# Row products of a Winograd convolution without column sums, with halved GpSimd sums and a planner that knows of the shared SBUF port

## The chip, the cores and the metric

The kernel runs on one core of a Trainium2 chip. The metric is device time in microseconds, from several runs of the compiled program; the time before is 2768.17 us, the median of 3 runs that lie between 2763.59 and 2770.75. The profile is one execution on the chip; times in the text that look like 533.33 are microseconds from the start of its span. Engines are named as in the profile: PE is TensorE, PEld its weight loads, DVE is VectorE, ACT is ScalarE, POOL is GpSimd, and SP is the engine that issues most DMAs.

## The reference, cut to what matters

There are 4 images of 256 channels and 48 x 48 pixels, in fp32. Two layers follow each other, each added to its input.

```python
# layer 0
h   = relu(bn(conv3x3(group_norm(x)) + conv_b))      # 256 -> 256 channels
q,k,v = split(qkv_w @ h + qkv_b)                     # 8 heads of 32
a   = softmax(q.T @ k * 32**-0.5) @ v                # over all 2304 pixels
x   = x + proj_w @ a + proj_b
# layer 1
g   = group_norm(x)
guidance = conv3x3(g, W_cat)                         # 45 channels
outs = [g]
for i, d in enumerate((1, 6, 12, 24, 36)):
    w = softmax(guidance[:, 9*i:9*i+9], axis=1)      # one 3x3 filter per pixel
    outs.append(sum(shift(g, d, tap) * w[:, tap] for tap in range(9)))
y   = W_scale @ concat(outs)                         # 1536 -> 256 channels
x   = x + batch_norm(y)                              # statistics over all images
```

## The kernel before, in words

**Stages.** The program first runs the conv and the q, k, v products of image 0 alone. Then, for each image, it runs the attention (some 350 us), and after it a stage in which layer 1 of this image (`dynamic_filters`, L1429 on) and the conv and q, k, v products of the next image are interleaved on TensorE. After image 3 layer 1 runs with work left over from image 2 in place of a next conv (`late`), and then the output is normalized and written. In the profile the interleaved stages are about 508 to 819, 1174 to 1486 and 1842 to 2154 us, and the last stage begins at about 2503.

**Order of instructions.** The order on every engine is the order in which the Python code issues instructions; nothing is moved later. To find a good order the code keeps a planner, `clock` (class `Clock`): an estimated time for each engine, advanced by an assumed duration at each instruction. `drive` holds several generators (the steps of layer 1) with a due time for each, and issues the first one that is due; where none is due it takes one step of the generator `other`, the next image's conv, if the time in `need[0]` has come. `run(ns)` takes conv steps worth that many nanoseconds. `either` puts a sum on DVE or POOL, whichever the planner expects to be done first; `moved` does the same for a copy on ACT or DVE.

**The conv.** Image 0 uses `conv`: rows are transformed by Winograd's F(4,3) down the columns of the image, which leaves six row products i = 0..5, each a matmul sum over 2 input halves and 3 horizontal taps. Images 1 to 3 use `Blocks` and `conv_blocks`: the same six row products, in the order `ORDER = (1, 2, 3, 4, 0, 5)`, and within each one F(2,3) along the row. So a tile (i, o), with o an output half, has four column products j of 2 matmuls each, 288 columns wide (L1139). Their inputs are column sums made by `along` from the row sums `v[i]` (four sums of 576 elements per partition for each i); those of rows 1, 2 and 3 are put on POOL, those of 4, 0 and 5 on either engine. The row sums `v[i]`, 1200 elements per partition, are all made by POOL (`sum`, L979): those of rows 1 and 2 in `stage0`, issued as the attention ends, the others in the generator `rest`. After each tile the four products are put together out of PSUM: ACT copies the first to `one`, DVE makes `two` with the second, and the third and fourth are added, by DVE from PSUM or by ACT and either engine. `after` adds pairs of row products, and ACT applies the batch norm and relu into `hid`. The transformed weights are made once, under image 0's conv (`Made`), stored in DRAM (`u_d`) and read a tile at a time by SP into one of three ring buffers (`taken`).

**End of the attention.** The exponentials `p` of a unit of queries are summed for the softmax by DVE (`acc`), a part of them by accumulating DMAs (`extra`). In the last unit of an image DVE adds `extra` to `acc` at step 15 and the exponentials of step 16 after that; the last step's go to TensorE directly. `close` sums `acc` over the partitions on TensorE, DVE makes reciprocals of them (two transposes) and scales the result, and `project` multiplies the last chunk by `proj_w` (L1412, tile `pp`). Only for image 3 are five idle "warm" matmuls issued between.

**Start of layer 1.** DVE adds the residual to `pp` and takes statistics, TensorE sums them over groups, and `gn` is normalized in place, half of the channels by DVE (L641) and half by ACT (L1963). Ahead of that ACT loads the square root's table, and after the square root the exponential's.

**Layer 1, per chunk of 8 rows.** `weights` makes the softmaxed filters; `far` does the four large dilations as matmuls with a banded matrix `amat`, which DVE fills by three predicated copies (L1660), from data that `own` and `xT` bring in order; `near` does dilation 1 by products on DVE, added up by POOL (L1759); `mixes` applies `W_scale` (L1854).

Of the kernel before, what the change touches and what calls it, by code (L numbers as in the profile page):

```python
# [17 lines left out]
P = 128  # L18
# [39 lines left out]
def conv_preact_kernel(  # L58
# [487 lines left out]
    with tc.tile_pool(name="w", bufs=1) as wpool, tc.tile_pool(  # L546
# [145 lines left out]
        class Clock:  # L692
# [3 lines left out]
            def __init__(self):  # L696
                self.t = dict.fromkeys(("PE", "DVE", "ACT", "POOL"), 0.0)

            def __call__(self, engine, ns, *after):

                self.t[engine] = max(self.t[engine], *(a + 150.0 for a in after), 0.0) + ns
                return self.t[engine]

# [27 lines left out]
        STEPS = [(i, j) for i, _ in TILES for j in (1, 2, 0, 3)]  # L731

        def taken(t):

            i, o = TILES[t]
            at = 1024 * ((t + 2) % 3)
            u = ring[:, at : at + 1024]
            nc.sync.dma_start(out=u, in_=u_d[i, o])
            return u.rearrange("p (h j c) -> p h j c", h=NH, j=4)

        class Made:
# [20 lines left out]
            def convert(self):  # L762
# [5 lines left out]
                for o in range(NH):  # L768
                    t = four[:, at + NH * 4 * P * o : at + NH * 4 * P * (o + 1)]
                    f = t.rearrange("p (h j c) -> p h j c", h=NH, j=4)  # L770
                    of = self.u[i][:, :, :, o * P : (o + 1) * P]
# [179 lines left out]
        class Blocks:  # L951


            def __init__(self, b, gn):
# [19 lines left out]
                self.of = {1: v[:, :z]}  # L974
                pad = gn.rearrange("p h r w -> p (h r w)")
                self.pad = [pad[:, z * j : z * (j + 1)] for j in range(2)]
                self.end = {}
                self.passed = set()

            def sum(self, out, x, y, op):  # L980
                nc.gpsimd.tensor_tensor(out, x, y, op)
                return clock("POOL", 2800)

            def stage0(self):
# [3 lines left out]
                nc.scalar.mul(v[5], d[1], 4.0)  # L988
                self.sum(v[0], d[4], v[0], ALU.subtract)
                self.sum(v[5], d[3], v[5], ALU.subtract)  # L990
                self.sum(v[1], v[0], v[5], ALU.add)
                self.along(1)
                self.sum(v[2], v[0], v[5], ALU.subtract)
# [7 lines left out]
            def rest(self):  # L1001
# [3 lines left out]
                for out, x, y, op in (  # L1005
                    (3, d[4], d[2], ALU.subtract), (6, v[6], v[4], ALU.subtract),
                    (4, v[3], v[6], ALU.subtract), (3, v[3], v[6], ALU.add),
# [19 lines left out]
                for i, after in ((4, 2), (0, 3), (5, 4)):  # L1027
# [13 lines left out]
            def hidden(self, hid):  # L1041
# [3 lines left out]
                    {2: hid[:, :z], 3: hid[:, z:], 4: self.pad[0], 0: self.pad[1], 5: self.pad[0]}  # L1045
                )

            def along(self, i, js=(1, 2, 0, 3)):
# [3 lines left out]
                for j in js:  # L1052
# [3 lines left out]
                    if i in ORDER[:3]:  # L1056
                        nc.gpsimd.tensor_tensor(to, d[x], d[y], op)
                        self.end[i, j] = clock("POOL", 1400)
                    else:
                        self.end[i, j] = either(to, d[x], d[y], op)  # L1060

        def either(out, a, c, op, *after):

            part = 0.5 if len(out.shape) == 2 and out.shape[-1] == XN else 1.0
            if clock.t["POOL"] + 1400 * part <= clock.t["DVE"] + 1000 * part:
                nc.gpsimd.tensor_tensor(out, a, c, op)
                return clock("POOL", 1400 * part, *after)
            nc.vector.tensor_tensor(out, a, c, op)
            return clock("DVE", 1000 * part, *after)

        def conv_blocks(b, psum_tile, blocks, pool, hid):
# [6 lines left out]
            results, last = [], [0.0]  # L1078
# [16 lines left out]
            def before(i, o):  # L1095

                s12, d12, s34, d34 = (blocks.held[:, j, o] for j in range(4))
                if i == 0:
                    t = spare.pop(0)
                    axpy(t, s34, -4.0, s12)  # L1100
                    relu(o, 2, t, clock("DVE", 700))
                    either(s12, s12, s34, ALU.subtract)
                elif i == 5:
                    t = spare.pop(0)
                    axpy(t, d34, -2.0, d12)
                    relu(o, 1, t, clock("DVE", 700))
                    axpy(d12, d34, -8.0, d12)
                    clock("DVE", 700)

            def target(i, o):  # L1110

                if i in (1, 3):
                    return blocks.first[o]
                if i in (2, 4):
                    return blocks.held[:, 1 if i == 2 else 3, o]
                return spare.pop(0)

            def after(i, o, y):

                s12, d12, s34, d34 = (blocks.held[:, j, o] for j in range(4))  # L1120
                if i in (2, 4):
                    s, d = (s12, d12) if i == 2 else (s34, d34)
                    either(s, y, blocks.first[o], ALU.add)
                    either(d, blocks.first[o], y, ALU.subtract)
                elif i in (0, 5):
                    relu(o, i and 3, y, either(y, y, s12 if i == 0 else d12, ALU.add))
# [1251 lines left out]
```

## Time and profile before

| | |
|---|---|
| median of 3 runs | 2768.17 us (2763.59 to 2770.75) |
| the profiled execution | 2768.08 us, of which the span is 2766.3 us |
| busy in the span | PE 2596.0, DVE 2142.2, ACT 1796.7, POOL 741.7 us |
| PE in the interleaved stages | 287.11 of 311, 289.84 of 312, 285.68 of 312 us |
| PE in the last stage, 2503 to 2767 | 212.90 of 264 us |
| DVE in the interleaved stages | 208.42, 207.02, 226.25 us |
| POOL in the interleaved stages | 159.43, 159.31, 163.91 us |
| mean granted TensorE clock | 0.982 |

In the tables of the profile a line gives the source line, the engine, what is written and read, and after the bar the busy time, the mean duration in ns and the idle time of the engine just before, with what ended it. In a timeline the first two columns are start and duration in us; several like instructions may be merged into one row (x8), and a bracket gives the idle time before and what ended it. A matmul of the program stands as two matmul records.

### The profile page before, as it was taken

To read this page: it belongs to the slowest core of one execution; us is meant where nothing else is said; L and a number is where in the kernel's file an instruction comes from. 1 tells how busy PE (TensorE), PEld (TensorE's weight loads), DVE (VectorE), ACT (ScalarE), POOL (GpSimd) and SP (SyncE) were. 2 spreads that over 40 slices of the span, in tenths; PEclk is the share of its full clock that TensorE was granted. 3 is DMA by queue.
4 is the path that set the end of the run, shared out by engine and by line. 5 is a ranking of instruction groups with operands and counts; after the bars stand their busy time and mean duration, and the time that the engine had idled before them with its cause. 6 is when DMAs were issued, how large, how long until landed. Compare 5 with 4: busy or idle time off the path is not lost. (4 is left out here: it accounts for less than half of the span.)

```text
span 2766.3 us, 42026 instructions
## 1 busy us (share of the span) xinstructions
PE 2596.0 (94%) x16820; PEld 1089.6 (39%) x16820; DVE 2142.2 (77%) x2045; ACT 1796.7 (65%) x2242; POOL 741.7 (27%) x641
## 2 busy tenths in 40 slices
PE   6999999889999999988999999998999999999994
PEld 5632222455562222345554222244555222234452
DVE  7778888777739988858765988885876988885476
ACT  3478888633449988843346888883445988873244
POOL 5200100456420100065550001016654010000352
PEclk9999999999999999999999999999999999999997
DMA  4704444323242444422333444442335344442465
GB/s 172 219 18 98 109 98 103 81 69 99 78 92 58 105 99 95 109 77 76 89 70 67 92 98 102 99 94 71 86 83 133 93 93 100 94 92 63 118 180 183
DMA packets 135979, 273.64 MB, mean 99 GB/s; under 512 B 56040, under 2 KB 97936, under 8 KB 134880
## 3 DMA queue, kind: packets, MB, share of 16 engines
q0 software_dynamic: 25952, 135.74, 21.5%
q1 hardware_dynamic: 109824, 135.14, 18.4%
q8 instruction: 134, 2.20, 0.4%
q14 instruction: 69, 0.57, 0.1%
HBM read 112.12 MB, written 36.04 MB: 54 GB/s over the span
## 5 line engine op out<-in xcount | busy, mean ns | idle before, releaser
L1340 DVE TENSOR_TENSOR acc<-acc,p 128x2048 f32<-128x2048 f32 (+1 forms) x572 | 1061.2, 1855 | 122.7 <-ACT p L1304 73.1
L1304 ACT ACTIVATE p<-se 128x1536 f32<-128x1536 f32 x648 | 938.7, 1449 | 0.1
L1295 PE MATMUL so<-q,k 32*128 32x512 f32 (+1 forms) x1440 | 726.4, 592 | 19.6 <-ACT p L1303 18.9
L1295 PE MATMUL se<-q,k 32*128 32x512 f32 (+1 forms) x4320 | 735.0, 592 | 0.0
L1324 PE MATMUL num<-p,vT 128*32 128x512 f32 (+1 forms) x5760 | 706.2, 560 | 4.6 <-ACT p L1304 2.4
L1303 ACT ACTIVATE p<-so 128x512 f32<-128x512 f32 x648 | 388.4, 599 | 193.8 <-PE se L1295 82.8
L1759 POOL TENSOR_TENSOR near<-near,prod 128x768 f32<-128x768 f32 x192 | 351.8, 1833 | 357.2 <-DVE prod L1754 347.6
L1295 PEld LDWEIGHTS so<-q,k 32*128 32x128 f32 x1440 | 216.1, 183 | 535.0 <-ACT p L1303 496.3
L1324 PEld LDWEIGHTS num<-p,vT 128*32 128x32 f32 x5760 | 134.5, 108 | 479.2 <-issue 444.3
L1344 POOL DMA_DIRECT2D ring<-p x124 | 105.5, 851 | 779.8 <-ACT p L1304 464.8
L1754 DVE TENSOR_TENSOR prod<-wb,pad 128x768 f32<-128x768 f32 x192 | 181.7, 953 | 68.5 <-ACT wb L1741 48.9
L1854 PE MATMUL py<-far,wsc 128*128 128x384 f32 x704 | 234.5, 487 | 0.0
L1295 PEld LDWEIGHTS se<-q,k 32*128 32x128 f32 x4320 | 226.7, 183 | 5.4 <-ACT p L1304 4.1
L1741 ACT COPY wb<-ws 128x384 f32<-128x384 f32 x216 | 109.0, 509 | 174.7 <-DVE prod L1754 146.4
L1462 ACT COPY far<-far 128x512 f32<-128x512 f32 x92 | 97.4, 1105 | 143.4 <-PE far L1688 142.0
L1342 POOL DMA_DIRECT2D ring<-p x32 | 17.9, 558 | 640.8 <-ACT p L1304 481.5
L1854 PEld LDWEIGHTS py<-far,wsc 128*128 128x128 f32 x704 | 131.9, 190 | 89.8 <-issue 1.8
L1489 PE MATMUL pg<-pad,wcat 128*45 128x384 f32 x864 | 151.7, 498 | 3.5 <-ACT lg L1547 2.1
L1219 PE MATMUL pq<-hid,wqkv 128*128 128x384 f32 x384 | 130.2, 497 | 7.6 <-ACT hid L1089 5.4
L1688 PE MATMUL far<-amat,xT 64*128 64x256 f32 x576 | 86.0, 416 | 18.3 <-DVE amat L1660 18.3
L1219 PEld LDWEIGHTS pq<-hid,wqkv 128*128 128x128 f32 x384 | 73.6, 194 | 60.6 <-ACT hid L1089 7.0
L1340 DVE TENSOR_TENSOR acc<-p,p 128x2048 f32<-128x2048 f32 x36 | 82.3, 2285 | 19.6 <-ACT p L1304 19.6
(305 smaller groups left out, 2711.1 us busy)
## 6 DMA issues: line engine op xcount, KB each, us to landing
ring<-p POOLq DMA_DIRECT2D x156, 768.0 KB, 5.7
ws<-w_d SPq DMA_DIRECT2D x216, 192.0 KB
ring<-u_d SPq DMA_DIRECT2D x36, 512.0 KB
pad<-in_x SPq DMA_DIRECT2D x14, 1152.0 KB
xst<-in_x POOLq DMA_DIRECT2D x36, 192.0 KB, 3.6
x_d<-pad SPq DMA_DIRECT2D x36, 192.0 KB
u_d<-pad SPq DMA_DIRECT2D x12, 512.0 KB
y_d<-y SPq DMA_DIRECT2D x14, 384.0 KB
```

The source lines that it names most:

```text
L1219: nc.tensor.matmul(pq[:, :CH], wqkv[:, i, s, g * P : (g + 1) * P], hid[:, i, cols], start=(i == 0), stop=(i == NH - 1),)
L1295: nc.tensor.matmul(dst[:, at : at + n], k_[r, g, m * P : (m + 1) * P], q[r, g, q0 : q0 + n], start=True, stop=True,)
L1303: nc.scalar.activation(p[:, 0, :], s1, AF.Exp, scale=QS)
L1304: nc.scalar.activation(p[:, 1:, :], s3, AF.Exp, scale=QS)
L1324: nc.tensor.matmul(st["num"][r, at : at + n], vT[:, m, g * P + j * D : g * P + (j + 1) * D], p[:, j, at : at + n], start=(m == 0 and not s ...
L1340: nc.vector.tensor_tensor(st["acc"][:, js], other[:, js], p[:, js], ALU.add)
L1344: nc.gpsimd.dma_start(out=extra, in_=p[:, 1:], accum_op=ALU.add)
L1489: nc.tensor.matmul(pg[64 * s : 64 * s + NG, :CH], wcat[:, ii, k, :], shifted(ii, cc, k // 3 - 1, k % 3 - 1), start=(i == 0 and k == 0), st ...
L1741: nc.scalar.copy(pw[:, :CH], fetched[c, k][0])
L1754: nc.vector.tensor_tensor(prod.rearrange("p h (r w) -> p h r w", w=WW), wb, src, ALU.mult)
L1759: nc.gpsimd.tensor_tensor(cat, cat, prod, ALU.add)
L1854: nc.tensor.matmul(py[c][:, o, :CH], wsc[:, n * NH + i, o * P : (o + 1) * P], rhs, start=(n == 0 and i == 0), stop=(n == order[-1] and i = ...
```

## The change

- **Planner.** `Clock` remembers POOL's last sums and the last DVE instruction that excludes them. `alone` gives the time at which DVE can start such an instruction; `both` books it and pushes POOL's later sums back. `either`, a layer-1 softmax product, the copies of `own` and those into `amat` now use it.
- **Half sums.** POOL's row sums and its sums in `near` are issued as two instructions, one per channel half.
- **Whole rows.** For rows 1 and 2 (`WHOLE`) there are no column sums: a tile has two halves of the output, each 6 matmuls (2 input halves x 3 taps) straight from `v[i]`. ACT copies row 1's products to `first`; DVE makes row 2's sum and difference with them from PSUM. Their weights are three per tile instead of four. The row sum `v[3] = d[4] - d[2]` moves to the front of `stage0`. The other rows' column sums get other buffers, may begin one row product earlier, and row 3's may go to either engine; one relu of row 0 is held back because of that.
- **End of the attention.** In the last unit steps 16 and 17, `acc` and `extra` are all summed by TensorE; DVE's two last additions go. The warm matmuls are issued for every image.
- **Start of layer 1.** The normalization is issued in two halves with conv steps between; the exponential's table is loaded at the first `weights`. Three clears move from POOL to DVE. In the last stage the last `pp` lies in two banks of another pool.
- **amat.** The three predicated copies are issued together.

```diff
@@ Clock
+            def alone(self, *after):
+                at = max(self.t["DVE"], *(a + 150.0 for a in after), 0.0)
+                return next((end for start, end in self.sums if start <= at < end), at)
+
+            def both(self, ns, *after):
+                at = self.alone(*after)
+                self.t["DVE"] = at + ns
+                self.held = at, at + ns
...
@@ Blocks
             def sum(self, out, x, y, op):
-                nc.gpsimd.tensor_tensor(out, x, y, op)
-                return clock("POOL", 2800)
+                for h in range(NH):
+                    nc.gpsimd.tensor_tensor(out[:, h], x[:, h], y[:, h], op)
+                    end = clock("POOL", 1400)
+                return end
@@ stage0
+                self.sum(v[3], d[4], d[2], ALU.subtract)
                 self.sum(v[0], d[4], v[0], ALU.subtract)
                 self.sum(v[5], d[3], v[5], ALU.subtract)
-                self.sum(v[1], v[0], v[5], ALU.add)
-                self.along(1)
-                self.sum(v[2], v[0], v[5], ALU.subtract)
+                for i, op in zip(WHOLE, (ALU.add, ALU.subtract)):
+                    end = self.sum(v[i], v[0], v[5], op)
...
@@ along
-                    if i in ORDER[:3]:
-                        nc.gpsimd.tensor_tensor(to, d[x], d[y], op)
-                        self.end[i, j] = clock("POOL", 1400)
-                    else:
-                        self.end[i, j] = either(to, d[x], d[y], op)
+                    self.end[i, j] = either(to, d[x], d[y], op)
@@ either
-            if clock.t["POOL"] + 1400 * part <= clock.t["DVE"] + 1000 * part:
+            if clock.t["POOL"] + 1300 * part <= clock.alone(*after) + 900 * part:
...
@@ conv_blocks
+                    if whole:
+                        half = slice(TJ * j, TJ * (j + 1))
+                        pairs = [
+                            (u[:, h, kx], blocks.v[i][:, h, half, kx : kx + WW])
+                            for h in range(NH) for kx in range(3)
+                        ]
...
+                        if i == ORDER[0]:
+                            nc.scalar.copy(first, m)
+                        else:
+                            tt(blocks.held[:, 0, o, cols], m, first, ALU.add)
+                            tt(blocks.held[:, 1, o, cols], first, m, ALU.subtract)
...
@@ attention
-                if end and m == NT - 1:
-                    sums(u, p, True, False)
+                if end and m >= NT - 2:
+                    sums(u, p, m == NT - 2, m == NT - 1)
+                    if m == NT - 2:
+                        sums(u, state[u]["acc"], False, False)
+                        sums(u, extra, False, False, 1)
...
-                sums(u, state[u]["acc"], u < last, True)
-                if u == last and b == B - 1:
+                if u < last:
+                    sums(u, state[u]["acc"], True, True)
+                else:
                     busy(ps_a.tile([P, 512], F32, tag="one", name="warm"), 5)
@@ dynamic_filters
-                nc.gpsimd.memset(t, 0.0)
+                nc.vector.memset(t, 0.0)
...
+                    yield lambda: clock.t["DVE"] - AHEAD
                     for t in range(3):
-                        yield lambda: clock.t["DVE"] - AHEAD
                         nc.vector.copy_predicated(
...
-                    nc.gpsimd.tensor_tensor(cat, cat, prod, ALU.add)
-                    end = clock("POOL", 1800, end)
+                    for h in range(NH):
+                        nc.gpsimd.tensor_tensor(cat[:, h], cat[:, h], prod[:, h], ALU.add)
+                        end = clock("POOL", 920, end)
...
-            table(AF.Exp)
             norm.shift_of()
-            for h in range(NH):
-                t = inside(gn, h)
...
-            run(2500)
+            for part in range(2):
+                for h in range(NH):
+                    t = inside(gn, h, HH // 2 * part, HH // 2)
...
+                run((900, 1600)[part])
```

## The prediction

> **What bounds the kernel now.** I read the page first, then the busy time by stage, the waits of TensorE inside one stage, and the timelines around its longest waits.
>
> ```profile
> PE 2596.0 (94%) x16820; PEld 1089.6 (39%) x16820; DVE 2142.2 (77%) x2045; ACT 1796.7 (65%) x2242; POOL 741.7 (27%) x641
> ...
> 508.00:819.00 311.00, 287.11 (x1370) 169.29 (x1362) 208.42 (x261) 129.08 (x217) 159.43 (x95) 0.98 0.34 84
> 1174.00:1486.00 312.00, 289.84 (x1389) 170.04 (x1382) 207.02 (x261) 130.50 (x218) 159.31 (x95) 0.97 0.35 84
> 1842.00:2154.00 312.00, 285.68 (x1514) 160.47 (x1506) 226.25 (x266) 150.09 (x239) 163.91 (x99) 0.97 0.37 97
> ```
>
> The last three lines are the stages that the change touches most: the second layer of one image with the conv of the next poured into its gaps (columns: stretch, length, then busy PE, PEld, DVE, ACT, POOL). TensorE works 286 to 290 of 312 us, the others 67% at most. TensorE bounds these stages, plus some 24 us of waits in each. Added TensorE work costs its full time there; a removed wait gains its full time.
>
> ```profile
> PE far L1688 <- DVE amat L1660: 6.1, 1, 6.1
> PE pc L1139 <- ACT one L1154: 2.9, 1, 2.9
> PE pp L1412 <- DVE ao L1377: 2.8, 1, 2.8
> PE xa L1608 <- ACT own L1462: 2.4, 4, 1.2
> PE xa L1608 <- DVE own L1464: 2.4, 1, 2.4
> PE py L1854 <- POOL near L1759: 1.5, 1, 1.5
> PE den L1356 <- DVE acc L1340: 1.3, 1, 1.3
> ```
>
> These are TensorE's waits of 508 to 819. The same ones stand in the other two stages (amat 18.3 us in 3 waits over the run). Why amat is late is seen in VectorE's timeline, beside GpSimd's:
>
> ```profile
> 579.56 2.95 DVE L1068 TENSOR_TENSOR cv_v<-cv_q,cv_v 128x576 f32<-128x576 f32 x1
> 582.44 2.96 DVE L1068 TENSOR_TENSOR two<-one,two 128x288 f32<-128x288 f32 x1
> 585.32 1.00 DVE L1660 COPY_PREDICATED amat<-along_y,bmat 128x768 f32<-128x768 uint32 x1
> ...
> 578.87 3.03 POOL L981 TENSOR_TENSOR cv_q<-pad,cv_q 128x1200 f32<-128x1200 f32 x1
> 581.86 3.22 POOL L981 TENSOR_TENSOR cv_q<-cv_q,cv_v 128x1200 f32<-128x1200 f32 x1
> ```
>
> Two VectorE sums that take 0.76 and 0.45 us undisturbed took 2.95 us each, and each ended with a GpSimd sum. The third amat copy stood behind them, and TensorE behind it. At the start of the stage:
>
> ```profile
> 528.24 4.51 PE L1412 MATMUL pp<-ao,wp 128*128 128x384 f32 x8 [2.75 <-DVE ao L1377]
> 533.33 4.12 PE L1139 MATMUL pc<-cv_v,ring 128*128 128x288 f32 x14 [0.58 <-POOL cv_v L1057]
> 543.47 1.72 PE L1139 MATMUL pc<-cv_v,ring 128*128 128x288 f32 x6 [2.92 <-ACT one L1154]
> ...
> 2509.75 2.82 PE L1412 MATMUL pp<-ao,wp 128*128 128x384 f32 x8 [0.40 <-DVE ao L1377]
> ```
>
> The eight pp records take 4.51 us after a 2.75 us pause (5.46 and 4.38 in the next two stages), but 2.82 us for image 3, where "warm" matmuls fill the pause.
>
> **What the Trainium skill says.** "SBUF — State Buffer", section "Who interferes with whom": a VectorE instruction with two SBUF inputs and a GpSimd one that reads SBUF exclude each other for a whole instruction. The trace agrees (2.95 against 0.76 us). "TensorE: Matmul & The Clock Gate", section on the clock gate: after idling the array runs at half clock. Here pp starts follow at 0.64 us instead of 0.32 after 2.75 us of idling, so it agrees in kind. "ScalarE: Activation LUTs", section "What ACT_TABLE_LOAD costs": 1283 ns and a drain; here 1.28 us x12.
>
> **The change, part by part.** The sum is made against the profiled execution, 2768.08 us (span 2766.3 and 1.8 around it); the median of the runs is 2768.17, so nothing has to be carried over.
>
> 1. *Whole row products.* A tile of rows 1 and 2 has 2 halves x 6 = 12 matmuls of 288 columns instead of 4 x 2 = 8; two rows, two output halves: 16 more per image, 48 in all. A matmul stands as two records (576 for the 288 of L1139). 36 records took 9.30 us at 570.98, so one follows another after (9.30-0.41)/35 = 0.254 us. 96 x 0.254 = **+24.4 us** of TensorE. The same strided operand runs in image 0's conv (L935, 48 records in 12.0 us), so no dearer price is open. I charge all of it.
>
> 2. *What that takes off.* GpSimd loses eight column sums per image (4.52 us at 532.11, 5.63 at 540.64), 10.2 us. Rows 1 and 2 lose their four column-combining operations per output half, row 2 also keeps its sums but straight out of PSUM, about 8 us per image of VectorE, ScalarE or GpSimd. Neither bounds the stage: nothing by itself. It brings the later rows' inputs forward, and so the filler for TensorE. The smaller u_d tiles (3/4) and the lighter conversion under image 0's conv lie under TensorE too: nothing, up to 1 us if the conversion was waited for.
>
> 3. *Start of the stage.* (i) The last unit's sums go to TensorE in the last two steps: about 0.86 us each for p, acc and extra. The sums end near 524.8 instead of 525.48: 0.7 us here, less in the others, 1.5 in all; for image 3 nothing, -0.3 to +1. (ii) Warm matmuls in the 2.75 us pause: pp takes 2.82, so 1.7 + 2.6 + 1.6 = 5.9 us. (iii) Row 1's first matmul needs one half sum instead of a row sum and a column sum. GpSimd's order becomes v3, v0, v5, v1. v3 needs nothing from ScalarE and can start when the last scores are done (about 519, or 520.2 after VectorE's acc sum), 2.7 us of work in time that is idle today. Then v1's first half is ready at about 530, pp's new end. The 0.6 and 0.7 us waits go: 1 us. (iv) The Exp table load (1.28 + 0.20 us) leaves the queue ahead of the normalization and the 2.30 us normalization is halved, so row 1's PSUM copies are no longer behind both: 3 x 2.92 = 8.8 us, and 1.6 us of slow clock after it in the second stage (six pc records 2.52 against 1.72, twelve pg 3.00 against 2.16). The table load then stands before the pg copy, where ScalarE is idle for 3.75 us. The three memsets move from GpSimd (1.5 us) to VectorE before the residual sums, in the time in which pp runs. Together **18.8 us**.
>
> 4. *The account of the lock, half sums, amat copies in one go.* The amat wait (3 x 6.1) and its slow restart (far 2.08 against 1.13, the pc after it 0.6: 1.5 each) are 22.8 us. The three copies are issued together and the GpSimd work is earlier; I take three quarters, **17 us**; bounds 0 and 22.8. The own copy (1.47 us at 660.18, 0.48 undisturbed, behind column sums that stay whole) and ScalarE's own copy: 1.16 + 0.64 + 2.44 + 1.15 slow = 5.4 per image; I take a third, **5 us**; bounds 0 and 16. Half sums cost overhead: GpSimd sums of 768 and 1200 take 1.81 and 2.72, a fixed part of about 0.2 us (estimate from these two), 192 x 0.2 = 38 us of an engine that is busy 27%, so hidden; where TensorE waits for the last near sum (1.53 us), 0.2 us each.
>
> 5. *Last stage.* pp leaves the bank that the late products need: the 1.93 us wait at 2512 and ten pl records at 0.516 instead of 0.323 us: 3.7; the 0.75 us wait for the normalization in part. **4 us**.
>
> Sum: 24.4 - 18.8 - 17 - 5 - 4 = **-20.4 us**, to 2747.7; I say **2748**.
>
> **Rivals.** *All lock waits go* (chance 0.14): parts 4 and 5 in full, gains 18.8 + 22.8 + 16 + 4.5 = 62: -38, 2730. For it: GpSimd has 10 to 13 us less to do early. Against: the column sums that block the own copy are left whole.
>
> *A wash* (0.18): the layer-1 chain comes 6 us earlier and meets other GpSimd sums. Part 4 gives nothing: 18.8 + 4 - 24.4, +1.6, 2770. Against: all three stages stop at amat for the same visible reason.
>
> *Slower* (0.12): the lock waits stay and one more appears. The sums that the planner may put on either engine (row 3's column sums too, which were GpSimd's alone) go to VectorE more often, and halves make more encounters; one far or own step per image then stands behind them. Part 4 nil and 3 us per stage more: +1.6 + 9 = 2779. It decides from part 4 at zero and 2.3 us per stage of new waiting. For it: VectorE works 46 of 57 us in 700 to 757.
>
> **How the numbers follow.** The forecast's own case (0.56) runs from 2735 to 2764. Runs of this kernel differ by 0.3%, 8.3 us, so the same means 2760 to 2776. Faster: 0.14 + 0.56 for the forecast's part below 2760, less its upper edge (0.02) and plus a little of the wash: **0.70**; same **0.18**; slower **0.12**. The range for 8 in 10 leaves out the best of the first rival and the slower cases: **2728 to 2771**.
>
> **What would show it.** the conv matmul line with 672 records (576 now); pp below 3 us in all four stages; no L1154 wait near the normalization; amat's three copies adjacent and no far wait over 2 us; VectorE sums of 576 never near 2.9 us; TensorE's idle per interleaved stage near 10 us, its busy time 8 us higher. Wrong if the first conv matmul waits over 2 us for v1 (GpSimd starting at 522.3 as now), if an amat or own wait of 5 us remains, or if the conv's last rows run past the second layer, as they already do in the third stage (waits of 1.64 and 3.80 us at 2073 to 2079).

## The result, and the profile after

The changed kernel takes 2769.55 us in the median of its runs (2762.33 to 2772.88), the kernel before 2768.31 us beside it (2763.59 to 2770.75). The ratio is 1.0002 with an interval of 0.9994 to 1.001: no difference that can be measured. Forecast were 2748 us and a faster kernel. The profiled execution of the changed kernel is the slowest of its 12 (2772.88 us), so in the profiles the two kernels lie 4.8 us apart, in the medians 1.2.

The busy times of the profiled execution, first line of its page, and the three stages of the second layer (columns: stretch, length, busy PE, PEld, DVE, ACT, POOL; the stretches begin and end with the stages, so they differ a little from those of before):

```profile
PE 2623.3 (95%) x17002; PEld 1116.8 (40%) x17002; DVE 2100.6 (76%) x2036; ACT 1796.5 (65%) x2233; POOL 711.6 (26%) x805
```

```profile
508.00:822.00 314.00, 294.73 (x1422) 176.60 (x1416) 198.63 (x262) 127.05 (x213) 149.52 (x136) 0.98 0.34 82
1172.00:1490.00 318.00, 297.92 (x1537) 176.82 (x1534) 209.25 (x267) 133.88 (x218) 150.59 (x137) 0.98 0.35 84
1840.00:2162.00 322.00, 302.53 (x1626) 175.12 (x1624) 214.43 (x273) 150.00 (x239) 147.97 (x137) 0.95 0.37 95
```

TensorE is 27.3 us busier than before, and the stages are no shorter: from the last score of one image to the first score of the next, the three together take 889.6 us instead of 875.0. Each still holds some 19 us in which TensorE doesn't work. What it waits for there has changed. TensorE's waits in 508 to 822:

```profile
PE pg L1551 <- DVE pad L641: 6.6, 1, 6.6
PE pq L1271 <- ACT hid L1122: 4.0, 1, 4.0
PE pg L1551 <- ACT lg L1609: 2.6, 1, 2.6
PE pc L1184 <- ACT cv_k L1221: 1.6, 1, 1.6
PE far L1751 <- DVE amat L1723: 1.4, 1, 1.4
...
PE xa L1671 <- DVE own L1521: 0.5, 2, 0.3
PE pp L1469 <- DVE ao L1433: 0.4, 1, 0.4
```

The wait for amat, 6.1 us before, is down to 1.4, the own waits are nearly gone, and pp no longer waits. But four other waits stand in the list, and the first is at the place where the forecast saw its largest gain: the first conv matmul of the second layer (pg) waits 6.6 us for the normalized image. TensorE's timeline there:

```profile
527.98 2.82 PE L1469 MATMUL pp<-ao,wp 128*128 128x384 f32 x8 [0.39 <-DVE ao L1433]
530.64 3.56 PE L1184 MATMUL pc<-cv_k,ring 128*128 128x288 f32 x14
...
545.33 4.26 PE L1551 MATMUL pg<-pad,wcat 128*45 128x384 f32 x12 [6.59 <-DVE pad L641]
```

pp runs in 2.82 us and row 1 of the next conv follows with no wait for its sum, both as forecast. Then comes the hole, and the twelve pg records behind it take 4.26 us. In the kernel before, the same twelve took 2.17:

```profile
545.12 2.17 PE L1489 MATMUL pg<-pad,wcat 128*45 128x384 f32 x12
```

"TensorE: Matmul & The Clock Gate" of the Trainium skill, part 1 on the HAM clock gate, states that an idle array falls to half its clock; here the factor is 1.96 after 6.59 us, and the granted clock is 0.50 from 542.7 to 549.4.

Why the normalized image is late is seen on VectorE and GpSimd in the same stretch:

```profile
536.39 6.45 DVE L685 SCALAR_TENSOR_TENSOR gshift_n<-gmean_n,grstd_n 128x2 f32<-128x2 f32 x1
542.76 2.51 DVE L641 TENSOR_SCALAR pad<-pad,gmean_n,grstd_n 128x1152 f32<-128x1152 f32 x2
```

```profile
534.33 2.85 POOL L1015 TENSOR_TENSOR cv_v<-cv_v,cv_q 128x600 f32<-128x600 f32 x2
537.15 2.86 POOL L1015 TENSOR_TENSOR cv_q<-cv_k,cv_v 128x600 f32<-128x600 f32 x2
539.98 2.84 POOL L1015 TENSOR_TENSOR cv_k<-cv_k,cv_v 128x600 f32<-128x600 f32 x2
542.90 1.76 POOL L1099 TENSOR_TENSOR hid<-cv_k 128x576 f32<-128x576 f32 x1
```

The shift (128 x 2 numbers) took 0.16 us before; now it takes 6.45. VectorE and GpSimd of the kernel before:

```profile
539.65 0.16 DVE L685 SCALAR_TENSOR_TENSOR gshift_n<-gmean_n,grstd_n 128x2 f32<-128x2 f32 x1
```

```profile
549.23 2.73 POOL L981 TENSOR_TENSOR cv_v<-cv_v,cv_q 128x1200 f32<-128x1200 f32 x1
```

In the changed kernel, from 534.33 to 542.82 GpSimd makes six half row sums (v6, v4 and v3, for the later conv rows) with no pause between them; the shift comes in on the second. It ends when they end: at 542.82 the sixth is done, the next GpSimd instruction starts only at 542.90, and the shift is over between the two. In the kernel before, GpSimd was in its memsets at this time (539.30 to 540.68), and v6 came at 549.23, with four of the eight column sums that the change takes away still ahead of it. The other two stages of the changed kernel show the same hold (6.83 and 6.24 us at 1208.38 and 1882.60).

A sum over the profiled execution shows where it went. I took the starts and ends of the attention's score matmuls (so) and of the first pg from both traces; the third and fourth columns are two experiments told below:

| us | before | after | e2, sums held | e14, two orders |
|---|---|---|---|---|
| to the first score | 152.1 | 151.4 | 151.7 | 152.5 |
| three times: last score to first pg | 78.6 | 76.4 | 56.3 | 60.6 |
| three times: first pg to the next image's first score | 796.4 | 813.2 | 806.7 | 791.1 |
| four attentions | 1474.4 | 1473.3 | 1473.7 | 1467.5 |
| behind the last attention | 264.8 | 256.8 | 254.6 | 254.2 |
| span | 2766.3 | 2771.1 | 2742.9 | 2726.0 |

Put into these rows, the forecast had -18.0 for the start of the stages (part 3 without 0.8 us: of its 1.6 us of slow clock, half lies on the pg records and so behind the first of them), -4 for the last stage, and 24.4 - 17 - 5 - 0.8 = +1.6 for the rest. Measured are -2.2, -8.0 and +16.8. So two things have to be explained: 16 us missing at the start and 15 us too many in the rest.

### The profile page after: what moved, and what is told of

Its sections match the earlier page's. It is cut to its first block, busy times and chain, and to the rows that moved or that the text cites. A ratio compares the mean times of both kernels' runs of the same rounds, so it can differ in the third digit from the quotient of the medians.

```text
span 2771.1 us, 42452 instructions
## 1 busy us (share of the span) xinstructions
PE 2623.3 (95%) x17002; PEld 1116.8 (40%) x17002; DVE 2100.6 (76%) x2036; ACT 1796.5 (65%) x2233; POOL 711.6 (26%) x805
## 5 line engine op out<-in xcount | busy, mean ns | idle before, releaser
L1823 POOL TENSOR_TENSOR near<-near,prod 128x384 f32<-128x384 f32 x384 | 388.4, 1040 | 409.4 <-DVE prod L1817 407.6
L1551 PE MATMUL pg<-pad,wcat 128*45 128x384 f32 x864 | 156.9, 515 | 28.5 <-DVE pad L641 19.9
L1551 PEld LDWEIGHTS pg<-pad,wcat 128*45 128x45 f32 x864 | 58.7, 125 | 115.1 <-issue 81.7
```

Of the source, the lines that this page charges most:

```text
L1551: nc.tensor.matmul(pg[64 * s : 64 * s + NG, :CH], wcat[:, ii, k, :], shifted(ii, cc, k // 3 - 1, k % 3 - 1), start=(i == 0 and k == 0), st ...
L1823: nc.gpsimd.tensor_tensor(cat[:, h], cat[:, h], prod[:, h], ALU.add)
```

## The experiments

All of them compute the whole result. Ratios are to the kernel before on the same chip. "Changed kernel" is the one of the diff above.

**What holds the shift.** Theory A: only the shift's form is at fault, since it reads two operands from SBUF. Theory B: anything on VectorE that contends is held as long as GpSimd works without a pause. The first run changes the form, the second takes away what holds it.

e1 makes the shift from two instructions with one SBUF operand each:

```
-nc.vector.scalar_tensor_tensor(out=self.shift, in0=self.mean, scalar=-1.0, in1=self.rstd, ...)
+for h in range(NH):
+    nc.vector.tensor_scalar(self.shift[:, h : h + 1], self.mean[:, h : h + 1],
+                            self.rstd[:, h : h + 1], -1.0, ALU.mult, ALU.mult)
```

> The changed kernel, with only the normalization's shift made differently: two VectorE instructions with one SBUF tensor input and a per-partition scalar each, in place of one with two SBUF inputs. Theory A (the 128x2 instruction takes 6.3 us because its two SBUF inputs exclude GpSimd's sums and those come without a pause): it falls to 0.2 us, TensorE's wait for the normalization before the first pg falls from 6.6 to 1 to 4 us in each of three stages, the slow restart after it goes too, and the time is 2746 to 2760 us. Theory B (any VectorE instruction that reads SBUF waits there, whatever its inputs, until GpSimd pauses): the wait moves to the new instructions or to the first half of the normalization, 6 to 7 us remain, and the time is 2766 to 2772 us.

Measured: 2767.34 us, ratio 1.0001 (0.9992 to 1.001). VectorE's timeline of e1:

```profile
534.57 0.33 DVE L686 TENSOR_SCALAR gshift_n<-gmean_n,grstd_n 128x1 f32<-128x1 f32 x2
534.82 8.82 DVE L641 TENSOR_SCALAR pad<-pad,gmean_n,grstd_n 128x1152 f32<-128x1152 f32 x2
```

The shift is no longer held (0.33 us for two), and the hold has moved to the next instruction: the two halves of the normalization take 8.82 us, against 1.67 undisturbed (e2 below). Nothing is gained, as theory B had it. "SBUF — State Buffer", section "Who interferes with whom", states both: an instruction with one SBUF input does not contend, but tensor_scalar can enter a mode with two ports, and then does. That fits the two lines; which mode the instructions ran in no profile shows.

e2 makes GpSimd wait for VectorE's half of the normalization, by a copy of one element that stands ahead of the row sums:

```
                 run((900, 1600)[part])
+            if not alone:
+                held_up = small.tile([P, 1], F32, ...)
+                nc.gpsimd.tensor_copy(held_up, gn[:, 0, HH, WW : WW + 1])
```

> The changed kernel, with one added GpSimd copy of a single column that reads the last element of VectorE's normalized half, ahead of the generator's first row sum. It holds GpSimd's queue until the normalization is done; the rest is as in the changed kernel. Theory A (GpSimd's unbroken row sums are what holds the normalization up): the shift takes under 2 us, pg starts some 5 to 6 us earlier in each of three stages, GpSimd's later sums come some 3 us later without TensorE waiting for them; 2748 to 2760 us. Rival C (those sums are themselves what TensorE needs soon after): pg starts earlier, but waits of like size appear before the conv's third row or before the first far product; 2766 to 2775 us.

Measured: **2743.84 us, ratio 0.9913 (0.9899 to 0.9928)**, 22 us below the kernel before by the medians, and 4 us below the range written for theory A. VectorE, GpSimd and TensorE of e2:

```profile
535.80 0.16 DVE L685 SCALAR_TENSOR_TENSOR gshift_n<-gmean_n,grstd_n 128x2 f32<-128x2 f32 x1
535.91 1.67 DVE L641 TENSOR_SCALAR pad<-pad,gmean_n,grstd_n 128x1152 f32<-128x1152 f32 x2
```

```profile
537.65 0.19 POOL L2044 COPY held_up<-pad 128x1 f32<-128x1 f32 x1 [4.00 <-DVE pad L641]
537.79 3.15 POOL L1015 TENSOR_TENSOR cv_v<-cv_v,cv_q 128x600 f32<-128x600 f32 x2
```

```profile
538.08 2.72 PE L1551 MATMUL pg<-pad,wcat 128*45 128x384 f32 x12
```

GpSimd stands idle for 4.00 us, and pg starts 18.8 us after the last score in all three stages, without a wait. The start of the stages gains 22.3 us on the kernel before; the forecast's 18.0 are there once the sums are out of the way. Nothing else in the list of waits shrinks much, so 3 x 6.6 us of wait and the slow clock behind it are what the hold takes off.

e3 makes the conv's row sums whole again (the near sums stay halves):

```
-for h in range(NH):
-    nc.gpsimd.tensor_tensor(out[:, h], x[:, h], y[:, h], op)
+nc.gpsimd.tensor_tensor(out, x, y, op)
```

> The changed kernel with GpSimd's row sums whole again (2.7 us, one instruction), the layer-1 sums still halved. Theory D (halves leave no pause in which VectorE gets the port, whole sums do, as the single handover in the kernel before suggests): the 128x2 shift takes at most one sum, up to 2.8 us, the wait before pg falls below 4 us, 2755 to 2766 us. Theory E (an instruction of two elements does not get in between back-to-back sums of either size): the shift takes 5 us or more and the time stays at 2766 to 2776 us.

Measured: 2760.31 us, ratio 0.9972 (0.996 to 0.9983). The shift takes 2.40 us: it ends with the whole sum that runs when it arrives. So three sums of 2.8 us hold it less than six of 1.43 us. The length of the sums is thus not what decides. What differs is a pause: each of the three whole sums reads what the one before it wrote, or overwrites what that one read, and GpSimd's timeline shows 0.08 us between them. Of the half sums none depends on the one just before it, only on the one two before, and there is no pause. That the pause is what lets the shift in is a reading of these timelines, which e5 tests.

e5 keeps the halves and only changes their order, so that within a half each depends on the one just before it:

```
-(6, v[6], v[4], -), (4, v[3], v[6], -), (3, v[3], v[6], +)       each: half 0, half 1
+for h in range(NH): (6, 6, 4, -), (4, 3, 6, -), (3, 3, 6, +)     on half h
```

> The six half row sums that GpSimd makes first for a conv are put into another order: one half of the channels through all three sums, then the other, so that each sum reads what the one just before it wrote. Nothing is added and nothing is left out. If what lets VectorE in is the pause of some 0.08 us that GpSimd shows where a sum depends on the one just before it, the 128x2 shift is let in at the first boundary: at most 3 us instead of 6.45, the first conv matmul waits at most 4 us instead of 6.6, and the kernel takes 2755 to 2763 us. If the length of GpSimd's unbroken work alone decides, with or without pauses, the shift stays at 6 us and the time at 2766 to 2772.

Measured: **2750.80 us, ratio 0.9934 (0.9916 to 0.9951)**. VectorE and GpSimd of e5:

```profile
535.79 0.90 DVE L685 SCALAR_TENSOR_TENSOR gshift_n<-gmean_n,grstd_n 128x2 f32<-128x2 f32 x1
536.62 2.80 DVE L641 TENSOR_SCALAR pad<-pad,gmean_n,grstd_n 128x1152 f32<-128x1152 f32 x2
```

```profile
535.21 1.46 POOL L1047 TENSOR_TENSOR cv_q<-cv_k,cv_v 128x600 f32<-128x600 f32 x1
536.75 2.04 POOL L1047 TENSOR_TENSOR cv_k<-cv_k,cv_v 128x600 f32<-128x600 f32 x1
```

The first sum ends at 536.67 and the next begins at 536.75; the shift gets in there, after 0.90 us. The other two stages have the same (1.26 and 0.69 us). Nothing was added, removed or resized, and 17 us are gained on the kernel before, more than was expected. That is the clearest evidence that the order of these sums is the cause. That a pause is needed it does not show: in e9's second stage and in e4 the shift got in without one (last section).

e6 puts the three memsets back on GpSimd (one word: `nc.vector.memset` to `nc.gpsimd.memset`).

> The three memsets that clear the padded planes' spare elements go back from VectorE to GpSimd, where they were before the change. If their move is what brought the row sums onto the shift, this alone gives most of it back: shift under 3 us, 2748 to 2760 us. If the removed column sums and the half sums, which let GpSimd and VectorE reach this place with less in front of them, are what did it, the memsets end before the row sums start and the shift is still held 4 us or more: 2762 to 2772 us.

Measured: 2767.85 us, ratio 0.999 (0.9977 to 1.0003). The memsets run from 534.00 to 535.38, the six sums begin behind them, and the shift, at 536.28, is held for 7.56 us. So the memsets' move is not what did it. The sums come early because the work ahead of them on GpSimd is shorter: in e4 below, with the eight column sums back, v6 begins at 541.41, behind the shift. Whether moving v3 forward has a part in it was not tested.

**What the whole rows cost.** e4 takes rows 1 and 2 back to column sums (the list of whole rows is empty, and the old branches for these two rows stand again):

```
-WHOLE = ORDER[:2]
+WHOLE = ()
...
-((4, 1), (0, 2), (5, 3))
+((4, 2), (0, 3), (5, 4))
```

> The changed kernel without its whole row products: rows 1 and 2 again take column sums, with the buffers, the order of the column sums and the direct relu of the kernel before; v3 stays in front and all other parts stay. If added TensorE work costs its full time (the prediction's first step), this is 24 us below the changed kernel, 2742 to 2750 us, and TensorE's busy time is 24 us lower. If the earlier rows are what pays for it, it is within 8 us of the changed kernel, 2762 to 2775 us, with TensorE waiting for GpSimd's column sums in the first 60 us of each stage.

Measured: 2751.19 us, ratio 0.9939 (0.9922 to 0.9956). Alone this looks as if the whole rows cost 18 us. But the eight column sums are back on GpSimd too, and with them the shift takes only 0.63 us (0.92 and 0.88 in the other stages). e4 removes both the rows and most of the hold.

e7 is e4 with e2's hold; beside e2 it is to isolate the rows:

> The changed kernel with rows 1 and 2 of the conv made with column sums again, and with GpSimd's row sums held behind VectorE's normalized half, both at once. Beside the kernel that is only held (2743.8 us) it tells what the two whole rows cost once the held shift is out of the way. If their 24.4 us of TensorE count in full: 2716 to 2727 us. If TensorE would otherwise stand idle for the column sums, so that the rows pay for themselves: 2738 to 2752 us. In between, the share of the 24.4 us that column sums would have hidden is read off.

Measured: 2752.15 us, ratio 0.9946 (0.993 to 0.9963), against 0.9913 for e2: with the shift free, the whole rows are not dearer but 8 to 9 us cheaper. In the three stages e7 is 8.6 us shorter than e2 (854.4 against 863.0 us), not 24.4, although it has the 96 records less: its pg starts 25.6 to 27.2 us after the last score instead of 18.8. In the first stage the same 30 conv records stand ahead of pg in both, but in e7 TensorE waits 5.2 us among them: 2.34 for a column sum of row 1, 1.70 for ScalarE's copy and 1.19 for VectorE's sum. In three stages that is 15.9 us, about what is missing of the 24.4. And at the start of the last attention it loses 16 us. TensorE's waits of e7 in 2100 to 2140:

```profile
PE so L1353 <- ACT p L1361: 8.6, 1, 8.6
PE se L1353 <- DVE prod L1823: 4.5, 1, 4.5
```

With the column sums back, GpSimd's near sums of the third stage end late (at 2115.52, 8 us behind the attention's first score). The stores of layer 1's data to DRAM (`late_d`) are issued when they end, and the first exponentials stand behind these: ScalarE is idle for 11.22 us there until a store of `late_d` lands. Why the near sums come late was not traced; GpSimd itself waits for VectorE's products between them. e4 has the same stall (its last attention takes 384.9 us, the others 365.6 to 367.4).

**What costs 15 us in the rest.** Over the whole run, TensorE's waits for lg grew from 2.1 to 7.9 us, those for hid from 5.4 to 11.0, and those for cv_k from 0.7 to 3.5: 14 us together. The largest growth is that of lg, 2.6 us in each stage, 0.9 at most before. The chain to it begins with the three amat copies that the change issues in one go. VectorE, ScalarE and TensorE of the changed kernel:

```profile
576.49 4.95 DVE L1723 COPY_PREDICATED amat<-along_y,bmat 128x768 f32<-128x768 uint32 x3
581.35 0.28 DVE L1590 TENSOR_REDUCE mx<-pt 128x15 f32<-128x135 f32 x1
...
587.61 0.78 DVE L1601 TENSOR_TENSOR e<-e,sm 128x135 f32<-128x135 f32 x1
```

```profile
589.24 1.99 ACT L1519 COPY far<-far 128x512 f32<-128x512 f32 x2 [0.66 <-PE far L1751]
591.03 0.87 ACT L1519 COPY own<-pad 128x384 f32<-128x384 f32 x1
591.80 0.49 ACT L1609 COPY lg<-pw 128x384 f32<-128x384 f32 x1
```

```profile
592.34 4.12 PE L1551 MATMUL pg<-pad,wcat 128*45 128x384 f32 x24 [2.64 <-ACT lg L1609]
```

Behind the copies on VectorE stands the softmax of the next pair's weights (mx, e), and on it hang pw, lg and the next pg. The last link is ScalarE's: pw is done at 589.69, but the copies of the far products, of which TensorE now makes three before pg, and of own stand ahead of lg until 591.90. e9 is the changed kernel, with no hold, and the copies put off one by one again:

```
-yield lambda: clock.t["DVE"] - AHEAD
 for t in range(3):
+    yield lambda: clock.t["DVE"] - AHEAD
     nc.vector.copy_predicated(amat, ...)
```

> The changed kernel, without the hold, with the three predicated copies put off one by one again. In the held kernel this gave 15.7 us (2743.8 to 2728.2). If issuing the three together costs that whether or not the shift is held, the waits for lg (2.6 us in each stage) shrink below 1 us here too and the time is 2750 to 2758 us. If it was an effect of the held kernel's own order of work alone, the time is 2764 to 2772 us.

Measured: **2750.81 us, ratio 0.9939 (0.9925 to 0.9953)**. VectorE and TensorE of e9:

```profile
573.96 1.03 DVE L1723 COPY_PREDICATED amat<-along_y,bmat 128x768 f32<-128x768 uint32 x1
...
576.53 0.28 DVE L1590 TENSOR_REDUCE mx<-pt 128x15 f32<-128x135 f32 x1
...
577.79 3.71 DVE L1723 COPY_PREDICATED amat<-along_y,bmat 128x768 f32<-128x768 uint32 x2
```

```profile
585.68 2.17 PE L1551 MATMUL pg<-pad,wcat 128*45 128x384 f32 x12 [0.78 <-ACT lg L1609]
```

The max now stands between the first and the second copy, and pg starts 68.1 us after the stage's last score instead of 72.4, ahead of the last two far products instead of behind all three. The wait for lg falls from 7.9 us in the whole kernel to 2.2. The wait for amat does not come back (1.9 us in all). In this execution the shift was held 6.32 and 6.18 us in two stages, but only 1.12 us in the second, where pg waits 2.78 us for the normalized image instead of 6.98; so a part of the 17 us may not be due to the copies. The held kernel is free of that.

e8 does the same to the held kernel:

> The held kernel (2743.8 us), with the second layer's predicated copies put off one by one again, each behind its own look at VectorE's account, as before the change. If issuing the six together is what took the 6 us wait for them away, the wait comes back in three stages: 2755 to 2764 us. If the account that leaves the lock out and the work taken off GpSimd did it, the wait stays at 2 us or less: 2741 to 2748 us.

Measured: **2728.17 us, ratio 0.9857 (0.9839 to 0.9875)**, 15.7 us below e2. Neither expectation had the time; the wait for amat stayed away (1.9 us in all), as the second had it. The two faults are independent in the kernels with whole rows, and e14, which has both cures by order alone (e5's order of sums, e9's copies) and no instruction more than the changed kernel, confirms it:

> The changed kernel with two things put into another order and nothing added: the first six half sums go through one half of the channels and then the other, and the predicated copies are put off one by one. If the two faults are independent, their gains add: 2769.6 - 18.8 - 18.7 = 2732, 2726 to 2738 us. If the second only used time that the first had freed, 2742 to 2752 us.

Measured: **2727.78 us, ratio 0.9866 (0.9845 to 0.9886)**. Its column of the table has 18 us less than before at the start of the stages, 5 less in the rest, 7 less in the attentions and 11 less behind the last one. TensorE's waits of e14 over the run:

```profile
PE pg L1552 <- DVE pad L641: 4.1, 3, 1.7
...
PE far L1752 <- DVE amat L1724: 2.8, 3, 0.9
PE pg L1552 <- ACT lg L1610: 2.1, 3, 0.7
```

**What the single means of part 4 are worth.** Three runs start from e8 and take one thing away each. e10 makes the near sums whole again (`nc.gpsimd.tensor_tensor(cat, cat, prod, ALU.add)`, booked at 1800 instead of twice 920):

> The held kernel with the copies put off one by one (2728.2 us), and the second layer's near sums made whole again: 192 sums of 768 columns instead of 384 of 384. If the halves are what keeps VectorE's copies out of long waits, the amat or own waits come back, 5 us or more in a stage: 2738 to 2755 us. If GpSimd's earlier work and the account do it, the halves are worth nothing or cost their overhead: 2722 to 2732 us.

Measured: 2739.11 us, ratio 0.9891 (0.987 to 0.9912). The halves are worth some 10 us, but not at amat (2.8 us of wait in all, 1.9 in e8): the waits for own go from 1.7 to 4.9 us and those for row 3's and later rows' partial sums (two) from 0.5 to 6.1.

e11 makes the conv's row sums whole again (e3's edit on e8):

> The held kernel with the copies put off one by one (2728.2 us), and the conv's row sums made whole again. With the normalization held clear of them, if half sums are worth something here, as the prediction had it, the time rises to 2735 us or more, since each wait of VectorE can be 2.8 us instead of 1.4, and the first conv matmul waits for a whole sum. If whole sums with their pauses let VectorE in sooner than unbroken halves, 2718 to 2726 us. Between these the size of the sum does not matter.

Measured: 2724.80 us, ratio 0.9841 (0.9822 to 0.9859). The interval overlaps that of e8: once the normalization is clear of them, these runs show no difference between whole and half row sums.

e13 takes the account of the lock away: a VectorE instruction is booked at its engine's own time, and no sum is put off for it:

```
 def alone(self, *after):
     at = max(self.t["DVE"], *(a + 150.0 for a in after), 0.0)
-    return next((end for start, end in self.sums if start <= at < end), at)
+    return at
 def both(self, ns, *after):
-    ...
+    return self("DVE", ns, *after)
```

> The held kernel with the copies put off one by one (2728.2 us), with the account that leaves the lock out taken away: the same costs, but a VectorE instruction is booked at its engine's own time and no sum is put off for it. The amat wait went from 6.1 us to at most 2 us in every run so far, whether the copies came together or not, near sums whole or not, column sums there or not. If the account is what removed it, it comes back here, 4 us or more in two stages at least, and the time is 2740 to 2760 us. If the shorter work of GpSimd ahead of it did, the wait stays below 2 us, and the time is 2722 to 2734 us.

Measured: 2748.46 us, ratio 0.9932 (0.9914 to 0.995). The account is worth 20 us, but again not at amat, which does not appear among the waits. The conv's own handovers carry it. TensorE's waits of e13 over the run (in e8: one 1.4, cv_v 2.4, no cv_k of VectorE):

```profile
PE pc L1175 <- ACT one L1196: 9.4, 6, 1.9
...
PE pc L1175 <- DVE cv_v L1192: 5.8, 3, 1.9
PE pc L1175 <- DVE cv_k L1219: 4.7, 4, 2.9
```

Both theories written for e13 missed: the time rose as one had it, the wait stayed away as the other had it.

e12 is e8 with rows 1 and 2 made with column sums again:

> The held kernel with the copies put off one by one (2728.2 us), and rows 1 and 2 made with column sums again. The earlier pair of held kernels gave the rows 8.3 us in favour of the whole ones, of which 16 us were one stall at the start of the last attention. If that stall is the order's accident, it is gone here, and the kernel gains what it saves in the stages, 8 to 10 us: 2716 to 2724 us. If the stall belongs to column sums (GpSimd's near sums end late in the third stage), it stays, and the time is 2730 to 2742 us.

Measured: 2762.58 us, ratio 0.9983 (0.9974 to 0.9992). Neither expectation held: the loss is 34 us. TensorE's waits of e12 over the run:

```profile
PE pc L1188 <- POOL pad L1102: 18.3, 3, 6.1
...
PE pc L1188 <- POOL cv_v L1093: 7.0, 3, 2.4
...
PE pc L1188 <- ACT one L1211: 5.0, 3, 1.8
```

The stall at the start of the last attention stays (383.2 us): all three kernels with column sums have it, and none of the others. The waits for cv_v, at row 1, are those of e4 and e7 too (7.0 and 7.1 us). The wait of 6.1 us in each stage is new. It stands some 130 us behind the last score and is for a column sum of a later row (4, 0 or 5) on GpSimd. e12 differs from e7 in the copies alone, and here putting them off one by one costs 10 us (0.9946 to 0.9983), where it gained 15 to 17 with whole rows. So the order of the copies and the column sums are not independent. In this kernel the whole rows earn 34 us instead of costing 24. One rival is untested: in e4, e7 and e12 v3 still stands in front, 3.6 us of GpSimd's time ahead of row 1's sums, which in the kernel before it did not.

## Why the prediction was wrong, by its own steps

**Part 3, start of the stage: step (iv) failed; the rest held.** pp took 2.8 us in all stages (the warm matmuls gained 5.9 us, as forecast), it began 0.5 to 1.1 us earlier after the last score, row 1 started without a wait, and L1154's 2.92 us wait is gone. But the normalization's gain of 8.8 + 1.6 us was worked out with the GpSimd work of the kernel before beside it. The same part moved v3 forward, part 2 took 10.2 us of column sums away per image, and part 4 cut the row sums into halves that follow each other without a pause; so the next GpSimd work, v6, v4 and v3, arrived exactly at the shift, and held it. Part 2 said of this only that it "brings the later rows' inputs forward". The halves have a share in it: with whole row sums the wait before pg is 12.2 us in three stages (e3) instead of 19.9. The hold cost 3 x 6.6 us of waiting and the half clock behind it; e2 and e5 give 25 and 19 us back (by their ratios). The listed sign ("wrong if the first conv matmul waits over 2 us for v1") looked at the first matmul of row 1; it was pg, and for the normalized image.

**Part 4: right about amat and own, wrong about the copies in one go.** The amat waits went from 18.3 to 5.5 us and the own waits from 14.6 to 4.6: 12.8 and 10 us, against 17 (with the slow clock) and 5. The copies in one go were counted among the means of this gain. They were a loss of 15.7 us on e2 and of about 17 us on the changed kernel (ratios 1.0002 and 0.9939): the step didn't name what stands behind the three copies on VectorE, which is the softmax that the next pg hangs on. The account (20 us) and the half near sums (10 us), which the prediction did not price one by one, are worth something on e8, but at other places than amat. One reading behind this part was loose: the two VectorE sums of 2.95 us did not end with a GpSimd sum, but 0.6 and 0.3 us after one.

**Parts 1 and 2: the records are right, the sign is not.** The conv lines hold 672 records, as said. "I charge all of it" (24.4 us) set against "nothing by itself" for what they replace was wrong: on the held kernel the whole rows gain 9 us, on e8 34. In the kernel before, TensorE waited 1.3 us in all for column sums; that they would become a bound when everything around them is moved forward could not be read from that row, and shows in e4, e7 and e12 (7.0 to 7.1 us at row 1, and 18.3 more in e12). Nor were the other engines busy for "67% at most": VectorE works 226 of the 312 us of the third stage, 73%.

**Part 5** was mis-sized: the last stage gained 8.0 us, not 4. Of these 3.7 lie before its first pg (22.6 to 18.9 us after the last score); what gained the other 4.3 was not traced.

The sum of -20.4 was thus not far from what the change holds without the first fault (e2: -22 us), but by luck: part 1 was too dear and part 4 hid a loss. Without both faults it holds -38 us (e14). The measured time is that of the rival called a wash, and half of its mechanism: the chain of layer 1 did come earlier and meet other GpSimd sums. But it had part 4 give nothing, whose two waits shrank by 22.8 us; the loss came at the normalization and behind the copies.

**Open.** Which term removed the amat wait is not settled: it stayed at 2.1 us or less at each place with the copies together or single, near sums whole or half, row sums whole or half, column sums back, and without the account. Several of them seem to be enough alone; no run took all away. The wait for hid at the conv's end (5.4 us before, 11.0 after, 12.7 in e8, 12.0 in e14, 7.5 in e7) was not traced further.

## What to carry to other kernels

When work is taken off an engine that shares a lock, look up what comes next in its queue and what then stands beside it: a shortened GpSimd queue put six ready sums onto a chain that had been free. Smaller pieces are not by themselves a shorter hold: six halves in a row held the shift for 6.45 us, whole sums with pauses between them for 2.40. Two cures worked here in all three stages: to order the pieces so that each depends on the one before, and to hold them behind the short chain. Before instructions are issued in one go to end a wait, name what waits behind them in that queue.

## What the runs showed of the hardware

I had expected a blocked VectorE instruction to get in when the running GpSimd instruction ends. That is how I read "SBUF — State Buffer", section "Who interferes with whom": the one that issues first has the ports for its whole instruction, and the other blocks. The 6.45 us of the shift is more than that: it was passed over at four ends of a half sum where the next followed at once, and got in at the fifth, where GpSimd paused for 0.08 us; so in all three stages (6.45, 6.83, 6.24 us). With pauses of that size between sums it got in at the first (0.90, 1.26, 0.69 us in e5; 2.40, 2.35, 2.39 us in e3).

A pause is not needed every time. In the second stage of e9 the same shift met the same half sums, with no pause between them, and got in at the first end:

```profile
1199.84 1.12 DVE L685 SCALAR_TENSOR_TENSOR gshift_n<-gmean_n,grstd_n 128x2 f32<-128x2 f32 x1
```

```profile
1198.06 2.88 POOL L1015 TENSOR_TENSOR cv_v<-cv_v,cv_q 128x600 f32<-128x600 f32 x2
1200.88 3.41 POOL L1015 TENSOR_TENSOR cv_q<-cv_k,cv_v 128x600 f32<-128x600 f32 x2
```

And between column sums, which follow each other without a pause too, it got in at the first end in all nine stages of e4, e7 and e12 (0.63 to 1.06 us). Other instructions do the same: of 135 VectorE instructions in the changed kernel's trace that took over 0.25 us longer than their shortest like, 116 were passed over at no end of a GpSimd instruction, and 47 of these got in where the next followed without a pause. What sets the held shifts apart from those is open. Only one execution of each kernel was profiled, so how often the shift is held is not known.
